# Tying all products of a four in order, and placing the attention steps ahead of other work, in a two-layer transformer kernel

## The chip, the cores and the metric

The kernel runs on one core of one Trainium2 chip. The metric is the device time of one execution in microseconds (us). TensorE is called PE below, its weight loads PEld, VectorE is DVE, ScalarE is ACT, GpSimd is POOL and the queue that starts most transfers is SP.

## The reference, cut to what matters

Two layers work on x of shape (4, 512, 128): four batch rows of 512 tokens with 128 channels, all float32. Each layer adds an attention and a mixture of experts to x, both fed by the same layer norm. Layer 0 has a banded attention (window 64) and 16 gated experts. Layer 1, which the change touches, is this:

```
def _L1_attn_ref(x, w_qkv, w_out):            # x = xn, 16 heads of 8 channels
    q, k, v = split(x @ w_qkv), each to (b, heads, n, 8)
    attn = softmax(q @ k^T / sqrt(128))
    out  = (attn @ v), heads put side by side
    return out @ w_out

def _L1_ffn_ref(x, ...):                      # 8 experts, top 2
    gate = softmax over the two largest scores of relu(x rw1 + rb1) rw2 + rb2
    out  = sum over experts e of gate_e * (relu(x W1_e + b1_e) W2_e + b2_e)

xn = layernorm(x)
x  = x + _L1_attn_ref(xn, ...) + _L1_ffn_ref(xn, ...)
```

## The kernel before, in words

**Layer 0** (`band_logits`, `gated_experts`, `prepare`) fills about the first 946 us. Its banded attention output of the last batch row (`band_values`, lines 304 to 374) and layer 1's experts of the last two batch rows (`relu_experts`, lines 392 to 451) are still to be done then. They run beside layer 1's attention.

**Layer 1's attention** (`full_attention`, lines 769 to 947) handles 16 groups: 4 batch rows times 4 groups of 4 heads. A head has only 8 channels, so each head of a group sits on its own 32 of the 128 rows of PE (q and k tiles of 128 partitions, head h at partitions 32h). Four products that lie on four different sets of 32 rows can be worked on side by side. For a group there are 4 token tiles of 128 rows; each (group, tile, two heads) is a pair, 128 pairs in all. Each pair is needed twice:

- as an "m" product (`score<-k,q`, line 920): q times k, of which DVE takes the row maxima over 128 x 1024 numbers (`nmax`, line 936);
- as an "x" product (`score<-qa,k`, same line): k times q with the negated maxima folded into q (`qa`), of which ACT takes exp over 128 x 1024 numbers (`ex`, line 942).

A step holds one m pair and one x pair, which use complementary head pairs, so that its four products lie on four row sets: this is a four. The x pair lies `AHEAD` = 12 pairs behind the m pair. So there are 6 steps with only m products, 116 mixed steps and 6 with only x products. The first product of a step waits (a Sync dependency) for the maxima and the exp of the step in front, whose PSUM banks it writes.

After every second step `weigh` (line 832) multiplies ex with the values, again four products, here on four column sets (`accbank<-ex,vaug`, line 838). Between the steps lie `queries` and `keys` (lines 810 and 819), `with_maxima` and `normalise` (transposes at line 792), `values`, `turned`, `project_out`, and the experts: `hidden` (line 381, then relu on ACT at line 389), the second expert product (line 442), `part` on DVE (446) and `total` on POOL (447).

**What sets the order.** The kernel is written in program order, and `weave` interleaves the attention with the other track in a fixed ratio of steps. When the program is built, a planner puts the instructions on each engine's queue: on each engine it takes, among those it holds to be ready at that moment of its model, the one with the lowest number, and the number is the place in program order. `tc.high_priority(offset=4000)` lowers the number of what is written inside by 4000. Layer 0's products at line 574 have that already. A manual dependency of class NoSync fixes the order on a queue and adds no wait; one of class Sync adds a wait. The queue that results is fixed; the engine works through it in order.

Before the change the helper `in_order(mm, new)` ties only the first product of a four to the last product that was written before it. The other three of the four are free to be placed whenever the planner picks them. The list `pace`, which `in_order` appends to, also ties each `hidden` product behind the attention product written last.

Of the kernel before, what the change touches and what calls it, by code (L numbers as in the profile page):

```python
# [23 lines left out]
AF = mybir.ActivationFunctionType  # L24
ALU = mybir.AluOpType
AX = mybir.AxisListType
PSUM = bass.MemoryType.PSUM

P = 128
B, T, C = 4, 512, 128  # L30
NT = B * T // P
TPB = T // P
# [65 lines left out]
def two_layers(ctx: ExitStack, tc: tile.TileContext, w: dict, consts: bass.AP, out: bass.AP):  # L98
    nc = tc.nc
# [10 lines left out]
    def accbank():  # L110
        return ps_acc.tile([P, 512], FP, tag="acc", name="accbank")
# [648 lines left out]
    vaug = [one.tile([P, TPB, H, 32], FP, name=f"vaug{i}") for i in range(2)]  # L760
    nmax = [one.tile([P, TPB, 4, 32], FP, name=f"nmax{i}") for i in range(2)]
    for i in range(2):
        nc.gpsimd.memset(vaug[i], 0.0)
        nc.gpsimd.memset(vaug[i][:, :, :, 8:9], 1.0)
        nc.gpsimd.memset(nmax[i], 0.0)

    AHEAD = 12

    def full_attention():
# [4 lines left out]
        inv = 1.0 / math.sqrt(float(C))  # L774
        groups = [(b, g) for b in range(B) for g in range(4)]
        outs, q, k, qa, av, ex = {}, {}, {}, {}, {}, {}
        freed = []
        last = pace

        def in_order(mm, new):  # L780
            if new and last:
                tc.add_manual_dep(
                    mm.ins, last[-1].ins.name,
                    mybir.DependencyInfo(mybir.DependencyClass.NoSync, mybir.DependencyReason.DATA),
                    reason="products of four tiles stay together",
                )
            last.append(mm)
# [44 lines left out]
        def weigh(n, i):  # L832
            b, g = groups[n]
            if i == 0:
                av[n] = accbank()
            for h in range(4):
                r = 32 * h
                mm = nc.tensor.matmul(  # L838
                    av[n][r:r + 32, :], vaug[b % 2][:, i, g * 4 + h, :], ex[n, i][:, h, :],
                    start=(i == 0), stop=(i == TPB - 1),  # L840
                )
                in_order(mm, h == 0)
            if i == TPB - 1:
                avs = work.tile([P, TPB, P], FP, tag="avs1", name="avs1")
                nc.scalar.copy(avs.rearrange("p t n -> p (t n)"), av[n])
                av[n] = avs
# [34 lines left out]
        pairs = [(n, i, two) for n in range(len(groups)) for i in range(TPB) for two in (0, 2)]  # L881
        steps, head = [], AHEAD // 2
        for j in range(head):
            steps.append((pairs[2 * j:2 * j + 2], []))
        m_step = {j: j // 2 for j in range(AHEAD)}
        x_step = {}
        for j in range(AHEAD, len(pairs)):
            x_step[j - AHEAD] = m_step[j] = len(steps)
            n, i, two = pairs[j - AHEAD]
            steps.append(([pairs[j]], [(n, i, 2 - pairs[j][2])]))  # L890
        for j in range(len(pairs) - AHEAD, len(pairs), 2):
            x_step[j] = x_step[j + 1] = len(steps)
            steps.append(([], pairs[j:j + 2]))

        for n, (b, g) in enumerate(groups):
            t = m_step[8 * n]
            at(t - 5 if n > 1 else t - 3, queries, n)
            at(t - 3 if n > 1 else t - 2, keys, n)
            if g == 0:
                at(t + 1, values, b)  # L900
            at(m_step[8 * n + 7] + 1, with_maxima, n)
            for i in range(TPB):
                at(x_step[8 * n + 2 * i + 1] + 1, weigh, n, i)
            t = x_step[8 * n + 7]
            at(t + 3, normalise, n)
            if g == 3:
                at(t + 5, turned, b)
                at(t + 6, project_out, b)

        for t in range(min(todo), max(todo) + 1):  # L910
            ms, xs = steps[t] if 0 <= t < len(steps) else ([], [])
            tags = iter(("m", "x"))
            work_on = []
            before, freed = freed, []
            for kind, (n, i, two) in [("m", p) for p in ms] + [("x", p) for p in xs]:
                ps = ps_q.tile([P, 2, T], FP, tag=next(tags), name="score")
                for h in range(two, two + 2):
                    r = slice(32 * h, 32 * h + 32)
                    own, seen = (q[n], k[n]) if kind == "m" else (k[n], qa[n])
                    mm = nc.tensor.matmul(  # L920
                        ps[:, h - two, :], own[r, i * P:(i + 1) * P], seen[r, :], start=True, stop=True
                    )
                    new = not work_on and h == two
                    in_order(mm, new)
                    if new:

                        for f in before:
                            tc.add_manual_dep(
                                mm.ins, f.ins.name,
                                mybir.DependencyInfo(mybir.DependencyClass.Sync, mybir.DependencyReason.DATA),  # L930
                                reason="products of four tiles stay together",
                            )
                work_on.append((kind, n, i, two, ps))
            for kind, n, i, two, ps in work_on[::-1]:
                if kind == "m":
                    freed.append(nc.vector.tensor_reduce(  # L936
                        nmax[n % 2][:, i, two:two + 2, 8:9], ps, AX.X, ALU.max, negate=True
                    ))
                else:
                    if (n, i) not in ex:  # L940
                        ex[n, i] = ep.tile([P, 4, T], FP, tag="ex", name="ex")
                    freed.append(nc.scalar.activation(ex[n, i][:, two:two + 2, :], ps, AF.Exp, scale=inv))  # L942
            for f, args in todo.get(t, []):
                f(*args)
            if t % 2:
                for _ in range(1 + (t % 8 in (1, 7))):
                    yield

    x_out = out.rearrange("b (t p) c -> p b t c", p=P)
    weave(  # L950
        (full_attention(), 106),
        (after(woven((band_values(B - 1, ready[B - 1][1]), 14), (experts[B - 2], 41)), relu_experts(B - 1)), 13 + 40 + 76 + 4),
    )
# [35 lines left out]
```

## Time and profile before

| | us |
|---|---|
| three runs | 1382.46, 1379.99, 1385.32 |
| median | 1382.46 |
| the profiled execution | 1381.3 |
| its span, first to last instruction | 1379.5 |

The profile covers one execution. Busy shares of the span are PE 85%, PEld 33%, DVE 73%, ACT 74%, POOL 7%. Layer 1's attention begins with the first m product at 946.7 us and the last x product ends at 1366.7 us.

How to read it: each product of the program is two passes on PE, so one product of 512 columns gives two MATMUL records of about 0.6 to 0.7 us. Records overlap, since PE is pipelined; what a pass takes from the stream is the distance from its start to the start of the next. "x2" in a timeline row means two records merged, and the number in front is the time that they cover. The bracket at the end of a row is the idle time of that engine just before it, and what ended it. PEclk is the clock that PE was granted, 1.00 being full speed.

### The profile page before, as it was taken

What the parts mean: (1) busy time and instruction counts of PE and PEld (TensorE: products, weight loads), DVE (VectorE), ACT (ScalarE), POOL (GpSimd) and SP (SyncE); (2) the same over time, 40 slices, a digit from 0 to 9 for tenths busy, and PEclk for the clock granted to TensorE, in tenths of its full rate; (3) what the DMA queues carried; (4) which work ended last, traced back from release to release, by engine and by line L of the source; (5) the groups of instructions that cost most, each with busy time, mean ns of one, the idle gap of its engine ahead of it and who ended that gap; (6) DMA issues with size and microseconds to landing.
All of it is one profiled execution on the core that took longest, in us unless ns stands there. A gap on an engine that the chain in (4) does not pass through costs nothing.

```text
span 1379.5 us, 17426 instructions
## 1 busy us (share of the span) xinstructions
PE 1174.3 (85%) x6763; PEld 450.2 (33%) x6763; DVE 1012.4 (73%) x1085; ACT 1018.5 (74%) x1160; POOL 96.9 (7%) x68
## 2 busy tenths in 40 slices
PE   5676976678889789889989988887999899999997
PEld 2122323123433323353333334232333332333322
DVE  4999998999866999987799998843444434444451
ACT  4899997999968899988889988862454435545554
POOL 2000000000000002200002320012000000000000
PEclk9799998899879999999999999999999989999999
DMA  7121213446212445622244751235133200011100
GB/s 268 44 74 52 76 52 103 100 118 153 62 41 75 150 102 145 170 64 64 73 153 110 180 131 48 67 96 166 49 88 77 69 9 24 24 38 39 31 16 8
DMA packets 168524, 117.61 MB, mean 85 GB/s; under 512 B 66621, under 2 KB 149274, under 8 KB 166906
## 3 DMA queue, kind: packets, MB, share of 16 engines
q1 hardware_dynamic: 166970, 109.77, 29.3%
q0 software_dynamic: 1184, 6.29, 1.2%
q8 instruction: 54, 0.88, 0.3%
q10 hardware_dynamic: 288, 0.43, 0.1%
q14 instruction: 28, 0.23, 0.1%
HBM read 89.00 MB, written 27.46 MB: 84 GB/s over the span
## 4 chain that ended last, share of the span: by engine, by line
PE 59%; ACT 17%; DVE 13%; DMA 6%; issue 5%; SPq 0%; DVEq 0%; ACTq 0%
PE score L920 11%; PE lbank L574 10%; PE bank L381 8%; PE bank L442 7%; ACT z L566 6%; DVE z L560 5%; PE accbank L838 4%; ACT z L562 3%; PE gbank L674 3%; PE accbank L663 3%; DMA wb<-by_s 3%; PE gbank L681 2%; DMA wT<-wT_all 2%; DVE nmax L936 2%; PE abank L810 1%
## 5 line engine op out<-in xcount | busy, mean ns | idle before, releaser
L560 DVE TENSOR_TENSOR z<-proj 128x2044 f32<-128x2044 f32 (+31 forms) x256 | 554.1, 2189 | 29.0 <-PE lbank L574 12.6
L574 PE MATMUL lbank<-z,place 128*32 128x504 f32 (+18 forms) x2048 | 288.9, 639 | 110.1 <-ACT z L566 68.8
L936 DVE TENSOR_REDUCE nmax<-score 128x2 f32<-128x1024 f32 x128 | 156.3, 1225 | 182.3 <-PE score L920 180.1
L566 ACT ACTIVATE z<-z,posb 128x1024 f32<-128x1024 f32 (+31 forms) x256 | 267.3, 1097 | 10.2 <-DVE z L560 8.2
L942 ACT ACTIVATE ex<-score 128x1024 f32<-128x1024 f32 x128 | 130.3, 1023 | 159.7 <-PE score L920 159.7
L562 ACT ACTIVATE z<-z,brep 128x2048 f32<-128x2048 f32 (+31 forms) x128 | 241.4, 1906 | 5.3 <-DVE z L560 4.9
L920 PE MATMUL score<-k,q 32*128 32x512 f32 x512 | 152.2, 655 | 13.9 <-DVE nmax L936 11.7
L447 POOL TENSOR_TENSOR total<-total,part 128x512 f32<-128x512 f32 x32 | 82.6, 2580 | 1038.3 <-DVE part L446 1038.3
L920 PE MATMUL score<-qa,k 32*128 32x512 f32 x512 | 139.7, 648 | 2.1 <-ACT ex L942 2.1
L381 PE MATMUL bank<-xT,ew 128*128 128x512 f32 x256 | 136.2, 626 | 1.6 <-ACT h L389 0.8
L442 PE MATMUL bank<-h,ew 128*128 128x512 f32 x256 | 133.1, 619 | 4.7 <-issue 4.7
L389 ACT ACTIVATE h<-bank,cols 128x512 f32<-128x512 f32 x144 | 97.1, 684 | 45.3 <-PE bank L381 44.6
L574 PEld LDWEIGHTS lbank<-z,place 128*32 128x32 f32 x2048 | 43.0, 112 | 264.2 <-ACT z L566 143.9
L663 PEld LDWEIGHTS accbank<-wT,lin 128*128 128x128 f32 x512 | 72.2, 204 | 60.4 <-issue 34.6
L663 PE MATMUL accbank<-wT,lin 128*128 128x128 f32 x512 | 82.1, 297 | 10.1 <-DVE lin L661 10.1
L674 PE MATMUL gbank<-tT,wT 128*128 128x512 f32 x128 | 72.2, 647 | 17.4 <-DMA wT<-wT_all 16.5
L838 PE MATMUL accbank<-ex,vaug 128*32 128x512 f32 x512 | 70.8, 619 | 0.2 <-ACT ex L942 0.2
L681 PE MATMUL gbank<-tT,wT 128*128 128x512 f32 x128 | 70.6, 635 | 0.0
L920 PEld LDWEIGHTS score<-k,q 32*128 32x128 f32 x512 | 41.2, 187 | 89.0 <-ACT ex L942 44.1
L442 PEld LDWEIGHTS bank<-h,ew 128*128 128x128 f32 x256 | 44.2, 193 | 74.4 <-issue 71.0
L381 PEld LDWEIGHTS bank<-xT,ew 128*128 128x128 f32 x256 | 41.9, 192 | 72.8 <-issue 43.6
L659 DVE SCALAR_TENSOR_TENSOR lin<-lin,r 128x512 f32<-128x512 f32 x64 | 44.5, 695 | 28.6 <-ACT lin L683 28.3
(188 smaller groups left out, 1193.7 us busy)
## 6 DMA issues: line engine op xcount, KB each, us to landing
r<-route SPq DMA_DIRECT2D x96, 256.0 KB, 3.5
ew<-in_L_ffn_W SPq DMA_DIRECT2D x64, 256.0 KB, 3.4
wb<-by_s SPq DMA_DIRECT2D x32, 512.0 KB, 4.1
wT<-wT_all SPq DMA_DIRECT2D x48, 192.0 KB, 3.0
by_t<-e SPq DMA_DIRECT2D x8, 1024.0 KB
f<-by_t SPq DMA_DIRECT2D x128, 64.0 KB, 3.1
by_s<-g SPq DMA_DIRECT2D x16, 512.0 KB, 4.2
wb<-by_s SPq DMA_DIRECT2D x24, 256.0 KB, 3.6
```

The lines of the kernel that those rows point to most:

```text
L381: mm = nc.tensor.matmul(ph, wt[:, c * P:(c + 1) * P], xT[:, b * T:(b + 1) * T], start=True, stop=True)
L442: nc.tensor.matmul(py, old[1][:, c, :], old[0][c], start=(c == 0), stop=(c == 3))
L560: nc.vector.tensor_tensor(z[:, :, :, 0:n], seen, own, ALU.subtract)
L562: nc.scalar.activation(z[:, :, :, 0:n], z[:, :, :, 0:n], AF.Gelu, bias=b_dmg)
L566: last = nc.scalar.activation(z[:, dq, :, 0:n], z[:, dq, :, 0:n], AF.Gelu, bias=posb[:, j:j + 1])
L574: mm = nc.tensor.matmul(ps[q:q + 32, t0:T], place[:, kind, 3 - dd:35 - dd], z[:, dq, hg, 0:n], start=(dd == 0), stop=(dd == 3),)
L663: nc.tensor.matmul(ya[:, i * P:(i + 1) * P], lin[:, i * P:(i + 1) * P], wT[:, 2, :], start=False, stop=(e == E0 - 1 and i == TPB - 1),)
L674: nc.tensor.matmul(pg, wT[:, 0, :], tT, start=True, stop=True)
L838: mm = nc.tensor.matmul(av[n][r:r + 32, :], vaug[b % 2][:, i, g * 4 + h, :], ex[n, i][:, h, :], start=(i == 0), stop=(i == TPB - 1),)
L920: mm = nc.tensor.matmul(ps[:, h - two, :], own[r, i * P:(i + 1) * P], seen[r, :], start=True, stop=True)
L936: freed.append(nc.vector.tensor_reduce(nmax[n % 2][:, i, two:two + 2, 8:9], ps, AX.X, ALU.max, negate=True))
L942: freed.append(nc.scalar.activation(ex[n, i][:, two:two + 2, :], ps, AF.Exp, scale=inv))
```

## The change

It does two things in `full_attention`. First, `in_order` ties every product, not only the first of a four, behind the product written just before it, for the scores and for `weigh`. Second, the score products, the `weigh` products, the maxima on DVE and the exp on ACT are written inside `tc.high_priority(offset=FIRST)` with `FIRST = 4000`. The Sync dependency of the first product of a step is left as it is. No instruction is added or removed.

```
+    FIRST = 4000
...
-        def in_order(mm, new):
-            if new and last:
+        def in_order(mm):
+            if last:
                 tc.add_manual_dep(
                     mm.ins, last[-1].ins.name,
                     mybir.DependencyInfo(mybir.DependencyClass.NoSync, mybir.DependencyReason.DATA),
...
-                mm = nc.tensor.matmul(
-                    av[n][r:r + 32, :], vaug[b % 2][:, i, g * 4 + h, :], ex[n, i][:, h, :],
-                    start=(i == 0), stop=(i == TPB - 1),
-                )
-                in_order(mm, h == 0)
+                with tc.high_priority(offset=FIRST):
+                    mm = nc.tensor.matmul(
+                        av[n][r:r + 32, :], vaug[b % 2][:, i, g * 4 + h, :], ex[n, i][:, h, :],
+                        start=(i == 0), stop=(i == TPB - 1),
+                    )
+                in_order(mm)
...
-                    mm = nc.tensor.matmul(
-                        ps[:, h - two, :], own[r, i * P:(i + 1) * P], seen[r, :], start=True, stop=True
-                    )
+                    with tc.high_priority(offset=FIRST):
+                        mm = nc.tensor.matmul(
+                            ps[:, h - two, :], own[r, i * P:(i + 1) * P], seen[r, :], start=True, stop=True
+                        )
                     new = not work_on and h == two
-                    in_order(mm, new)
+                    in_order(mm)
...
-                    freed.append(nc.vector.tensor_reduce(
-                        nmax[n % 2][:, i, two:two + 2, 8:9], ps, AX.X, ALU.max, negate=True
-                    ))
+                    with tc.high_priority(offset=FIRST):
+                        freed.append(nc.vector.tensor_reduce(
+                            nmax[n % 2][:, i, two:two + 2, 8:9], ps, AX.X, ALU.max, negate=True
+                        ))
...
-                    freed.append(nc.scalar.activation(ex[n, i][:, two:two + 2, :], ps, AF.Exp, scale=inv))
+                    with tc.high_priority(offset=FIRST):
+                        freed.append(nc.scalar.activation(ex[n, i][:, two:two + 2, :], ps, AF.Exp, scale=inv))
```

## The prediction

> **What bounds the kernel now.** The change touches nothing before 946.7 us, so I read that part by stage first: busy time per engine and granted clock in five stretches of layer 1's attention.
>
> ```profile
> core 0: us, PE busy (x) PEld busy (x) DVE busy (x) ACT busy (x) POOL busy (x), PEclk, DMA share, GB/s
> 946.00:970.00 24.00, 16.32 (x76) 6.49 (x77) 14.15 (x14) 3.69 (x6) 0.00 (x0) 0.86 0.51 128
> 970.00:1117.00 147.00, 136.90 (x935) 49.13 (x934) 70.72 (x90) 71.38 (x89) 3.83 (x3) 0.98 0.26 62
> 1117.00:1140.00 23.00, 21.88 (x73) 9.23 (x74) 5.85 (x16) 6.17 (x10) 0.00 (x0) 0.70 0.05 12
> 1140.00:1346.00 206.00, 202.00 (x1096) 64.88 (x1099) 101.13 (x106) 107.38 (x128) 8.89 (x7) 1.00 0.10 29
> 1346.00:1380.00 34.00, 24.39 (x146) 7.95 (x146) 5.08 (x9) 14.30 (x16) 1.28 (x1) 0.90 0.03 8
> ```
>
> From 1140 to 1346 PE is busy 202 of 206 us at full clock, DVE and ACT about half. A busy PE need not be at its peak, so I looked for what PE waits for there (the view of waits, PE alone, same stretch): apart from 0.6 us at one transpose, only this.
>
> ```profile
> PE score L920 <- DVE nmax L936: 3.5, 8, 0.9
> PE score L920 <- ACT ex L942: 0.7, 1, 0.7
> ```
>
> So this stage is bound by PE's stream: it gets shorter by what leaves the stream, not by an earlier maximum. What leaves the stream is seen in PE's timeline.
>
> ```profile
> 1204.02 0.70 PE L920 MATMUL score<-k,q 32*128 32x512 f32 x2
> 1204.03 0.70 PE L920 MATMUL score<-qa,k 32*128 32x512 f32 x2
> ...
> 1205.09 0.66 PE L792 MATMUL abank<-cst,o 128*128 128x128 f32 x4
> 1205.68 1.07 PE L838 MATMUL accbank<-ex,vaug 128*32 128x512 f32 x8
> 1206.67 1.12 PE L920 MATMUL score<-k,q 32*128 32x512 f32 x2
> 1207.72 0.66 PE L792 MATMUL abank<-cst,nmax 128*128 128x128 f32 x4
> 1208.31 0.69 PE L920 MATMUL score<-k,q 32*128 32x512 f32 x1
> 1208.32 0.70 PE L920 MATMUL score<-qa,k 32*128 32x512 f32 x2
> ...
> 1209.38 1.16 PE L868 MATMUL abank<-w_out,oT 128*128 128x128 f32 x8
> ```
>
> The four at 1204.02 holds the stream until 1205.09: 1.07 us. The next is split: one m product alone (1206.67 to 1207.72, 1.05 us), four transposes, then the other three (1208.31 to 1209.38, 1.07 us). A product alone costs as much as a four, so a split costs 1.05 us. The same timeline over the stage shows how a step closes when nothing is put behind `weigh`, and in the last steps, which have x products only:
>
> ```profile
> 1218.50 1.07 PE L838 MATMUL accbank<-ex,vaug 128*32 128x512 f32 x8
> ...
> 1219.98 0.70 PE L920 MATMUL score<-k,q 32*128 32x512 f32 x2 [0.41 <-DVE nmax L936]
> ```
>
> ```profile
> 1362.32 1.14 PE L920 MATMUL score<-qa,k 32*128 32x512 f32 x8 [0.72 <-ACT ex L942]
> ...
> 1363.56 1.94 ACT L942 ACTIVATE ex<-score 128x1024 f32<-128x1024 f32 x2 [1.29 <-PE score L920]
> ...
> 1365.55 0.71 PE L920 MATMUL score<-qa,k 32*128 32x512 f32 x4 [0.72 <-ACT ex L942]
> ```
>
> **The change part by part.** *Tying the four, with priority for its products.* Tying alone would not keep a stranger out; it is the priority that lets the second product win against an older transpose that becomes ready meanwhile. Going through PE's timeline from 946 to 1366 I find split fours at 953.97, 976.49, 1002.36, 1015.72, 1041.17, 1055.44, 1107.76, 1206.67 and 1303.57, each one product first and three later, and one in three parts at 1119.23, 1126.93 and 1131.15. Eight of the nine cost 1.05 each: 8.4. The one at 953.97 lies in the m-only steps, where the maxima set the pace; there the four transposes between (0.58) go too: 1.6. The one in three parts takes 2.01 (half clock) + 1.05 + 2.01 = 5.07 against 2.02 for a four at half clock: 3.0. Sum 13.0 us.
>
> *How much of it reaches the end.* Of the splits, only two lie in the stage that is PE from end to end. Six lie between 970 and 1117, where PE is idle 10 of 147 us, mostly in one wait of 4.34 us for a transfer of `band_values` (1083 to 1087); work saved ahead of it does not shorten the wait by itself, but the attention is then further on, and the experts behind it use the time. I count these at 80% of 13.0, 10.4; bounds 2.1 (the two alone) and 13.0.
>
> *Products placed earlier.* In the PE-bound stage the first m product starts a median of 0.58 us after its maximum ended, and never under 0.15: fours are late by about 0.4 us, because older work goes first. Moving the four forward saves no PE time; it moves fillers behind it. Its price is a wait. The row at 1219.98 shows it: with `weigh` alone between two fours, PE waits for the maximum (1.23) that began when the four ended. `weigh` takes 0.99 of the stream (1205.68 to 1206.67), so the four could have started at 1219.49 and starts at 1219.98: 0.49 lost. Behind the waiting product in PE's queue is everything else, experts first. Four steps of this stage look like that. How many there will be, this trace cannot show: none more, or all `weigh` groups that have something behind them now, 23 of the 35 of this stage and so about 42 of all 64, that is 0 to 20.6 us. I take 6 more, 2.9 us, because of a regularity: four transposes in front of `weigh` are followed by the four at once (7 of 7), `weigh` directly behind the four is followed by one more filler in 19 of 23 cases, and steps without `weigh` mostly have two fillers. The filling is nearly constant, about 1.6 to 2.1 us. That is how it looks if the planner takes the four when it is ready, and it needs no priority for that now.
>
> *Maxima and exp first.* DVE starts a maximum 0.05 us after its product, ACT an exp 0.14 us after (medians from 1140 to 1346). Nothing to gain; 0. What they pass is delayed by at most one of them: a relu (0.69) by an exp (1.02), `part` on DVE by a maximum (1.23), and POOL's `total` behind it. Cover: ACT and DVE are half idle, and POOL waits 254 us of this stage for `part` anyway. Without that cover a relu that is a microsecond late leaves a filler slot empty, 0.4 us; I put it into the 2.9.
>
> *SP and the loads.* No DMA is marked, but expert weights are asked for when their buffers come free, which now is up to one four (1.07) later. They are asked for about one expert (24 to 31 us) ahead and land in 3.4 us (the list of DMA issues): 0. If a load did become late, PE would wait with products queued behind it, as in the 4.34 us above; bound 6.
>
> *The clock.* Here a row and a rule differ. The trace: from 1113.4 to 1117.2 PE ran only six transposes, no gap over 1.06 us, and the products after it took 1.01 us a pass instead of 0.53, seven passes or so, about 3 us lost. The Trainium skill, "TensorE: Matmul & The Clock Gate", section "Why this matters for your kernels", asks only that no idle gap exceed about 3 us. By the rule nothing here would go cold, and earlier products could gain nothing; by the row, a four placed among the transposes and among the 26 small router products (1127.98 to 1131.15, after which a pass took 1.01 again) could keep the clock: up to 6 us. The row decides that the loss exists. Whether a four can be there is another thing: the exp it must wait for stands behind two table loads (1.28 each) for a square root until 1115.03. I take 1 of the 6.
>
> *The tail.* The last steps are ACT's: two exps, 3.22 us a step, and PE idle about 1.1 in each of three steps after the last expert product (1355). Attention further ahead leaves expert products to fill that; bounds 0 and 3.3, I take 1.5.
>
> Sum: −10.4 + 2.9 − 1 − 1.5 = −10.0 us, against the profiled execution's 1381.3 (span 1379.5): 1371.3. The median of the runs is 1.2 higher: 1372.5.
>
> **The rivals.** *Healed, but absorbed.* The splits go, but the six early ones shorten only waits for transfers and for the layer norm of the last row, so 2.1 to 4 us are left: 1379. For it: the stretch 970 to 1140 has chains of transfers (3.9% of the chain in layer 1 is `wb`). Against it: PE work from later is there to fill.
>
> *PE waits at the marked products* (slower). If the planner holds the next four to be ready while `weigh` still runs, priority now places it directly behind, in all of the 42 groups, and PE loses 0.49 in each: +20.6 − 10.4 = +10.2, 1393. It breaks even at 10.4 / 0.49 = 21 groups, and is slower by over 0.5% from 35. For it: four such steps exist. Against it: the regular filling above.
>
> *The ties split the fours.* If a tied product counted as ready only some time after the one in front, fillers would slip in after each: 128 fours by 1.05, +134 us. Against it: the first `weigh` product is tied to the four already, and in the PE-bound stage 23 groups follow the four directly.
>
> *The splits stay*, since something else than order holds the second product: 1382. Against it: in all ten the first product's Sync dependency had covered both banks.
>
> **How the numbers follow.** A measurement of this kernel can tell about 0.5%, 6.9 us, from no change. Main case 0.55, 1362 to 1377 on its own; absorbed 0.20; PE waits 0.17; ties split 0.03; splits stay 0.05. Faster by over 0.5%: 0.47 of the main case and 0.05 of the second, 0.52. Within 0.5%: 0.08 + 0.13 + 0.04 + 0.01, 0.26. Slower: 0.22. The range, from a main case with a clock gain at 1361 to most of the waiting case at 1392, leaves out about 2 in 10.
>
> **What would show it.** Right: every L920 group between 970 and 1346 has eight records together, none of two or six; the waits of L920 for the maxima stay near eight in the PE-bound stage; expert products stand in the gaps of the x-only steps. Wrong: many brackets of 0.4 us at L920, strangers inside the fours, a stretch of experts alone after the last x product, or a new wait of some us for `wb` or expert weights.

## The result, and the profile after

The changed kernel takes 1363.6 us (median of 4 runs) against 1381.2 for the kernel before beside it: ratio 0.9873, 95% interval 0.9835 to 0.9911. Two later comparisons, each on one chip with more runs, gave 0.9909 (0.9888 to 0.9930) and 0.9899 (0.9883 to 0.9914). So it is about 0.9% to 1.3% faster. The profiled execution took 1362.1 us, its span is 1360.3.

**Cut off what the change does not touch.** The two spans differ by 19.2 us, but not all of it is the change. Layer 1's attention begins with the first `queries` product (`abank<-xT,wqk`). It starts at 943.0 us before and at 936.1 after, although PE's queue is the same up to there. In the 13 profiled executions here that have this same queue, that moment lay anywhere from 935.9 to 943.5. What follows it, up to the end of the span, repeats much better. I call it the rest:

| kernel | rest, us, of each profiled execution |
|---|---|
| before | 436.5 |
| ties only (same queues as before) | 438.0 |
| changed | 424.2, 425.0, 424.3 |
| priority for products two to four only | 421.4, 422.2 |
| priority for score products only | 420.5, 421.4 |
| priority for score products only, `wb` products later | 418.8 |

So the change takes about 12 to 13 us off the rest (11.5 to 13.8 between single executions); the other 6 us or so between the first two profiles is the scatter of layer 0. The first two rows are the same program (experiment 1), so 1.5 us between them is scatter too.

The same five stretches as before, moved up by 6.9 us, since the attention starts that much earlier:

```profile
core 0: us, PE busy (x) PEld busy (x) DVE busy (x) ACT busy (x) POOL busy (x), PEclk, DMA share, GB/s
939.10:963.10 24.00, 16.54 (x78) 6.47 (x78) 15.34 (x14) 4.27 (x7) 0.00 (x0) 0.86 0.48 118
963.10:1110.10 147.00, 137.10 (x981) 49.71 (x980) 72.71 (x91) 74.22 (x91) 3.82 (x3) 0.98 0.25 62
1110.10:1133.10 23.00, 22.22 (x115) 8.62 (x108) 10.59 (x20) 10.79 (x14) 0.00 (x0) 0.80 0.04 12
1133.10:1339.10 206.00, 203.92 (x1076) 65.60 (x1072) 94.09 (x102) 107.08 (x128) 8.91 (x7) 1.00 0.09 29
1339.10:1360.30 21.20, 12.94 (x83) 4.72 (x82) 3.07 (x7) 7.52 (x10) 1.26 (x1) 0.97 0.04 13
```

Three things are to be seen. The same 147 us hold more matmul records (981 against 935): the attention is further on. The 23 us around the router have a clock of 0.80 in place of 0.70. The long stretch is PE from end to end as before, and the last stretch ends 12 us sooner (21.2 us against 33.5 to the end of the span): the end has moved, no engine has become faster.

What PE waits for in the long stretch (the view of waits, PE alone):

```profile
PE score L923 <- ACT ex L947: 0.7, 1, 0.7
PE score L923 <- DVE nmax L940: 0.7, 1, 0.7
PE score L923 <- DVE qa L831: 0.5, 1, 0.5
```

Eight waits for the maxima, 3.5 us, have become one of 0.7. And a new kind stands there: a wait for `qa`. PE's timeline shows what it is:

```profile
1190.91 0.70 PE L923 MATMUL score<-k,q 32*128 32x512 f32 x2
1190.93 0.70 PE L923 MATMUL score<-qa,k 32*128 32x512 f32 x2
...
1193.46 1.13 PE L923 MATMUL score<-k,q 32*128 32x512 f32 x4
1194.52 0.66 PE L793 MATMUL abank<-cst,nmax 128*128 128x128 f32 x4
1195.01 1.02 PE L442 MATMUL bank<-h,ew 128*128 128x512 f32 x2
1196.51 1.13 PE L923 MATMUL score<-qa,k 32*128 32x512 f32 x4 [0.47 <-DVE qa L831]
1197.56 1.06 PE L840 MATMUL accbank<-ex,vaug 128*32 128x512 f32 x8
```

At 1190.91 the four is whole. The next one is split in the middle: its m pair runs at 1193.46 alone, and its x pair must wait for `qa`, whose transposes (L793, of `with_maxima`) come only then. These transposes have no priority, so the products have overtaken the work that they need. There are four such splits (m pairs at 1055.14, 1142.39, 1193.46 and 1266.59); the ten of before are gone.

A late `qa` also costs time where no stranger comes between. Here the weight load of the x pair waits for it (the bracket at PEld), and PE with it:

```profile
1169.38 1.09 PE L923 MATMUL score<-k,q 32*128 32x512 f32 x3
...
1169.88 0.30 PEld L923 LDWEIGHTS score<-qa,k 32*128 32x128 f32 x4 [0.21 <-DVE qa L831]
1169.88 0.70 PE L923 MATMUL score<-qa,k 32*128 32x512 f32 x2
...
1170.94 1.06 PE L840 MATMUL accbank<-ex,vaug 128*32 128x512 f32 x8
```

This four holds the stream for 1.56 us (1169.38 to 1170.94) in place of 1.07. Five fours look like this (1169.38, 1219.22, 1243.31, 1293.84, 1317.06), 2.5 us in all. All nine places, the four splits and the five holds, are the first x pair of a group of heads, the first that needs the new `qa`. Together they cost 4.2 + 2.5 = 6.7 us.

**The ledger.** I summed the distances from the start of each matmul record to the start of the next, over the rest, and put what lies beyond a record's own end, less the 0.06 us by which records overlap when PE runs back to back, down as idle. The score products took 152.7 us of PE's stream before and 147.1 after, that is −5.6; everything else of the stream −3.0; idle time went from 36.4 to 32.7. Together −12.3. The −5.6 is the difference of two larger terms: −12.5 for the ten healed splits (experiment 3) and +6.9 for the late `qa`.

### The profile page after: what moved, and what is told of

It reads as the page before. It is cut to its first block, busy times and chain, and to the rows that moved or that the text cites. A ratio compares the mean times of both kernels' runs of the same rounds, so it can differ in the third digit from the quotient of the medians.

```text
span 1360.3 us, 17428 instructions
## 1 busy us (share of the span) xinstructions
PE 1161.7 (85%) x6763; PEld 447.2 (33%) x6763; DVE 1012.0 (74%) x1085; ACT 1019.6 (75%) x1160; POOL 96.9 (7%) x68
## 4 chain that ended last, share of the span: by engine, by line
PE 59%; ACT 17%; DVE 12%; DMA 6%; issue 6%; SPq 0%; POOLq 0%; POOL 0%; DVEq 0%
PE lbank L574 11%; PE score L923 10%; PE bank L381 8%; ACT z L566 7%; PE bank L442 7%; DVE z L560 5%; PE accbank L840 4%; PE gbank L674 3%; ACT z L562 3%; PE accbank L663 3%; PE gbank L681 2%; DMA wT<-wT_all 2%; DMA wb<-by_s 2%; DVE nmax L940 2%; PE bank L235 1%
## 5 line engine op out<-in xcount | busy, mean ns | idle before, releaser
L574 PE MATMUL lbank<-z,place 128*32 128x504 f32 (+18 forms) x2048 | 294.2, 649 | 106.7 <-ACT z L566 64.5
L923 PE MATMUL score<-k,q 32*128 32x512 f32 x512 | 141.0, 655 | 11.1 <-DVE nmax L940 8.4
L674 PE MATMUL gbank<-tT,wT 128*128 128x512 f32 x128 | 71.2, 639 | 16.1 <-DMA wT<-wT_all 15.4
L681 PE MATMUL gbank<-tT,wT 128*128 128x512 f32 x128 | 67.2, 607 | 0.0
L923 PEld LDWEIGHTS score<-k,q 32*128 32x128 f32 x512 | 38.3, 186 | 80.7 <-ACT ex L947 39.4
```

Of the source, the lines that this page charges most:

```text
L574: mm = nc.tensor.matmul(ps[q:q + 32, t0:T], place[:, kind, 3 - dd:35 - dd], z[:, dq, hg, 0:n], start=(dd == 0), stop=(dd == 3),)
L674: nc.tensor.matmul(pg, wT[:, 0, :], tT, start=True, stop=True)
L923: mm = nc.tensor.matmul(ps[:, h - two, :], own[r, i * P:(i + 1) * P], seen[r, :], start=True, stop=True)
```

## The experiments

**1. The ties alone.** All four `with tc.high_priority(offset=FIRST)` taken out of the changed kernel, `in_order(mm)` kept.

```
-                with tc.high_priority(offset=FIRST):
+                if True:
...   (the same at the other three)
```

> The change with its ties and without its priorities. Theory A (the priority heals the fours, a tie alone keeps no stranger out): the same as before, about 1381 us, with the ten split fours in the same places. Rival (the tie is what keeps the four together): the splits go and the time falls by 6.5 to 13 us, to about 1370.

Measured: 1377.0 against 1377.3, ratio 1.0 (0.9986 to 1.0014). As built, its queues are those of before, instruction for instruction, on all five engines. A tie says what comes after what, not that nothing may come between. The same comparison of the queues shows that priority for the maxima and exp alone, with the ties of before, also leaves every queue as it was, and that leaving these two out of the change gives the queues of the changed kernel. So of the change only the priority of the products acts, together with the ties. These two variants were compared as built and not run.

**2. The priority alone.** The changed kernel with the old ties (`in_order(mm, new)`, first products only).

> The change with its priorities and with the ties of before (only the first product of a four is tied). Theory A (healed fours are the gain, and priority needs the ties, since weigh and score products of equal rank can mix): groups of weigh or score products come apart in some 25 to 40 places at about 1.05 us each, so about 1385 to 1400 us. Rival (priority alone does it, the ties are idle): the time of the changed kernel, 1364.

Measured: 1409.7, ratio 1.0248 (1.0223 to 1.0273), 32 us slower than before, and slower than the 1385 to 1400 expected. PE's timeline at one of the bad places:

```profile
1238.78 1.04 PE L840 MATMUL accbank<-ex,vaug 128*32 128x512 f32 x2
1239.76 0.69 PE L923 MATMUL score<-k,q 32*128 32x512 f32 x1
1239.76 0.69 PE L923 MATMUL score<-qa,k 32*128 32x512 f32 x1
...
1240.81 1.05 PE L840 MATMUL accbank<-ex,vaug 128*32 128x512 f32 x2
1241.79 1.12 PE L923 MATMUL score<-qa,k 32*128 32x512 f32 x2
```

One `weigh` product alone (two passes, x2), two score products, one `weigh` product, one score product: each holds the stream for about 1 us, as a whole four would. When everything of a step has the same priority, the untied products of `weigh` and of the score mix. Elsewhere the four is only shuffled (m, x, m, x), and that costs nothing: it takes 1.08. Compared with the changed kernel, the score products take 28.2 us more of the stream and `weigh` 15.6, and the rest is 45.5 longer. So each half of the change needs the other; the rival, that the ties are idle, falls.

**3. Whole fours at their old places.** All products tied; only the second to fourth have priority, the first keeps its place in program order.

```
-                    with tc.high_priority(offset=FIRST):
+                    with tc.high_priority(offset=FIRST if work_on or h > two else 0):
                         mm = nc.tensor.matmul(
                             ps[:, h - two, :], ...
...
-                with tc.high_priority(offset=FIRST):
+                with tc.high_priority(offset=FIRST if h else 0):
                     mm = nc.tensor.matmul(
                         av[n][r:r + 32, :], ...
...   (maxima and exp without priority)
```

> Ties on all products; only the second to fourth product of each four has priority, the first one keeps its place in program order, and maxima and exp keep theirs. All fours are whole, but they start as late as before, behind older work. Theory A (the gain is the healed fours alone): ten splits at 1.05 and a little more, so 10 to 13 us less than before, about 1370, or a few us under that since no new split is made. Rival B (the gain is that whole steps are placed earlier, ahead of transposes and of the router): at most a third of the gain, 1376 or more.

Measured: 1361.2 against 1377.3, ratio 0.9886 (0.9867 to 0.9905). The rest is 421.4, the score products take 140.2 us of the stream: 12.5 less than before (11.2 in the second execution of this kernel), which is close to the prediction's price of the ten splits (13.0). The stretch of the new split in the changed kernel, in this one:

```profile
1191.67 0.70 PE L923 MATMUL score<-k,q 32*128 32x512 f32 x2
1191.68 0.70 PE L923 MATMUL score<-qa,k 32*128 32x512 f32 x2
...
1192.74 1.06 PE L840 MATMUL accbank<-ex,vaug 128*32 128x512 f32 x8
1193.74 1.12 PE L811 MATMUL abank<-xT,wqk 128*128 128x512 f32 x2
1194.79 0.70 PE L923 MATMUL score<-k,q 32*128 32x512 f32 x2
1194.81 0.70 PE L923 MATMUL score<-qa,k 32*128 32x512 f32 x2
```

Since the first product waits its turn in program order, `qa` is there when it runs, and all 128 fours are whole. Its waits for the maxima in the long stretch:

```profile
PE score L923 <- DVE nmax L940: 1.9, 5, 0.4
```

Rival B, that placing whole steps earlier makes the gain, falls: without any of that the whole gain is here. Nor does the changed kernel itself start its fours earlier: in its long stretch the first m product starts a median of 0.58 us after its maximum ended, which is what the prediction counted before the change.

**4. The changed kernel again**, unedited, beside these three.

> The changed kernel once more, on the same chip as the three others: 1364 us, 17 us under before. Its profile tells how much of the 6 us by which layer 0 ended earlier belongs to the run: if that is chance, layer 0 ends at other times here (928 to 936 us at the first product of layer 1's attention) by some us; if it is a property of the changed program, again near 936 against 943 before.

Measured: 1365.2 against 1377.3, ratio 0.9909. Layer 1 starts at 940.2 in its profile, 4.1 us later than in the first one of the same kernel; the rest is 425.0 against 424.2. The 6 us of layer 0 are chance.

**5. Splits made on purpose.** `weigh` does not run at its place but inside the next four, between the first product and the other three.

```
         def weigh(n, i):
+            held.append((n, i))
+
+        def weigh_now(n, i):
...
                     if new:
                         for f in before:
                             tc.add_manual_dep(
...
+                        while held:
+                            weigh_now(*held.pop(0))
```

> The changed kernel, with each weigh group moved from behind its four into the next four, between the first product and the other three: about 60 fours are split on purpose, nothing is added. It measures the price of a split. Theory A (a lone product holds the stream as long as a four, 1.05 us, and PE is the bound nearly everywhere): 60 x 1.05 = 63 us more than the changed kernel, about 1425. Rival (much of a split is hidden, because PE has waits to fill or the three others run beside their neighbours): 30 us or less, 1395 or under.

Measured: 1490.3 against 1378.1, ratio 1.0825 (1.0795 to 1.0856), about 125 us more than the changed kernel and twice what theory A expected, four times the rival's bound. The timeline has the form that was meant:

```profile
1209.08 1.12 PE L928 MATMUL score<-k,q 32*128 32x512 f32 x2
1210.13 1.06 PE L845 MATMUL accbank<-ex,vaug 128*32 128x512 f32 x8
1211.12 0.69 PE L928 MATMUL score<-k,q 32*128 32x512 f32 x1
1211.13 0.70 PE L928 MATMUL score<-qa,k 32*128 32x512 f32 x2
...
1212.19 1.12 PE L381 MATMUL bank<-xT,ew 128*128 128x512 f32 x2
```

The lone product takes 1.05 (1209.08 to 1210.13). 58 of them stand in the trace, 55 of them m products, and m products take 54.1 us more of the stream than in the changed kernel, about 0.98 each, a little more without the late `qa` that it has itself. That part is as theory A had it. But the rest is 130 us longer, and the other 76 us are not the price of a split. The second m product now comes after `weigh`, so the maximum, and with it the next four, starts 2 us later: PE's idle time in the rest grows from 32.7 to 67.6, that is 35 us. The other 41 us are in other products, no more in number but slower: PE runs at half clock for 114 us of the rest, against 27 in the changed kernel. Two kernels, the stretch from 1130 to 1330 of the changed one and from 1150 to 1350 of this one:

```profile
1130.00:1330.00 200.00, 198.72 (x1040) 63.97 (x1040) 95.22 (x105) 102.34 (x122) 8.91 (x7) 0.99 0.10 30
```

```profile
1150.00:1350.00 200.00, 184.62 (x774) 59.46 (x778) 71.60 (x85) 74.90 (x91) 5.08 (x4) 0.89 0.07 22
```

In these 200 us the granted clock is at half in six stretches of 3.4 to 13.7 us. Five of them begin 0.4 to 2.2 us after the end of a wait of 1.4 to 1.6 us; the longest, at 1153.0, begins at the end of the router's small products, with no wait in front. One of the five:

```profile
1189.73 0.49 PE L799 MATMUL abank<-w_qkv,xT 128*128 128x128 f32 x2 [1.55 <-DVE qa L831]
1190.15 1.73 PE L928 MATMUL score<-k,q 32*128 32x512 f32 x2
...
1194.69 1.06 PE L928 MATMUL score<-k,q 32*128 32x512 f32 x1
```

The passes from there on take 1.06 where others take 0.59, until 1200.8.

**6. More slack for `qa`.** `AHEAD = 14` in the changed kernel.

> The changed kernel with AHEAD = 14 in place of 12, so that the x products have one more step of slack behind with_maxima, whose transposes have no priority. One more step with m products only at the start, one more with x products only at the end. Theory A (the four fours that the change still splits are x pairs waiting for qa, which with_maxima delivers late, and cost 1.06 each): no split mixed four, 4.2 us less than the changed kernel, about 1360. Rival (the longer start and end, whose steps take 3.2 to 3.6 us against 3.0, eat it): 1364 or more.

Measured: 1367.3, ratio 0.9924 (0.9901 to 0.9946): not faster than the changed kernel. The step that was aimed at did happen: no mixed four is split (one is still held for `qa`, at 1063.68), and PE's stream is 4.2 us shorter (387.3 against 391.5). But idle time grew by 9.8 us. Half of it is a wait that was already there (view of waits, PE, from 963 to 1125 us; first the changed kernel, then this one):

```profile
PE bank L348 <- DMA wb<-by_s: 4.2, 1, 4.2
```

```profile
PE bank L348 <- DMA wb<-by_s: 9.1, 4, 4.3
```

Another 3.0 us is what the rival named, the longer end: from the first four with x products only to the end of the span it is 34.0 us here and 31.0 in the changed kernel. So the splits were worth about what theory A said, and two other costs ate it.

I read the longer wait so: the queue puts the products of `band_values` where the planner takes their transfer to have landed, and when the attention in front of them gets shorter, they stand at the head of PE's queue before their data. Experiment 12 tests only that more distance shortens the wait.

**7. `with_maxima` with a priority of its own**, behind the products and ahead of all else.

```
+            with tc.high_priority(offset=FIRST // 2):
                 pt = columns(nmax[n % 2].rearrange("p t h e -> p t (h e)"))
                 qa[n] = work.tile([P, T], FP, tag="qa", name="qa")
                 nc.vector.tensor_tensor(qa[n], pt, q[n], ALU.add)
```

> The changed kernel, with with_maxima (transposes and the sum into qa) at a priority of 2000, behind the products and ahead of all other work. If lateness in the planner's order alone splits the last four fours, they should all be whole: 4.2 us less. In the queue as built three of the four stay split, so what holds qa is not rank but the one abank bank or nmax itself: then 1 us less than the changed kernel, within its noise.

Measured: 1370.4, ratio 0.9946 (0.9925 to 0.9967), a miss: some 5 to 6 us slower than the changed kernel where 1 to 4 less was expected. The stream is 2.5 us shorter, idle time 8.1 longer: the waits for `wb` at L348 are 8.0 us, and PE now also waits for `nmax` with the transposes themselves (3.3 us, in three waits, at L793, from 963 to 1125). A likely reading is that a transpose of high rank is put in the queue as soon as the planner holds the maxima to be ready, and everything behind it waits when they are not. Three splits stand in this trace, but not all at the old places: two are where the changed kernel has them, the third where it only held the x pair, and one old split has become such a hold. Why these stay is open.

**8. Priority for the score products alone**, ties on all.

> Ties on all products, priority for the score products alone; weigh, maxima and exp keep program order. The score fours are all whole, some three weigh groups come apart, and the next four stands directly behind weigh in about twice as many places as before (29 against 15). Theory A with the price of the prediction (0.49 us of waiting where nothing lies between weigh and the next four, 1.05 for a weigh group that comes apart): -12 for the whole fours, +7 for 14 more waits, +3 for weigh, so 2 us under before. Rival (such waits cost nothing, since the work that is passed fills later gaps): 9 us or more under before.

Measured: 1360.4, ratio 0.9877 (0.9853 to 0.9902); the rival was right. The score products take 139.9 us of the stream, and `weigh`, of which three groups come apart, 69.4 (66.5 before): the −12 and the +3 of theory A are there. The +7 is not. The next four does stand directly behind `weigh` in 29 places, but in 27 of them other work has gone in front of `weigh`, so the maximum has had its time. Only in two does `weigh` stand alone between two fours, and there PE waits 0.47 us, as priced; the gaps in all 29 places sum to 1.9 us.

**9 to 12. Side by side on one chip.** The changed kernel, experiments 8 and 3 again, and experiment 8 with one pause more in `band_values`, in layer 1 only (the step counts given to `weave` are raised to match, from 14 to 22 and from 13 + 40 to 21 + 40):

```
                         in_=bass.AP(by_s.tensor, at, [[H * BW - 1, P], [BW, 8], [1, n]]),
                     )
+                if pace:
+                    yield
                 for g4 in range(2 * half, 2 * half + 2):
```

> The changed kernel on the same chip as the three others, so that they can be compared with it directly: 12 to 17 us under before.

> Priority for the score products alone, once more, beside the changed kernel. Theory A (the gain is whole fours; the changed kernel still splits four at about 1.05 and this one none): 4 us under the changed kernel. Rival (that difference came from the chips of the earlier calls): no difference over 2 us.

> Priority for the second to fourth product alone, once more, beside the changed kernel. If whole fours are all that counts, the same as score_prio_2 within 2 us and 4 us under the changed kernel, although here the fours keep their late places and there they do not.

> score_prio with one more pause of the program order between the loads of wb and the products that need them, so that these products stand further back in PE's queue. It asks what the wait of about 4 us in front of them costs, which all kernels so far have near 1080 us: with the half-speed passes after it about 6 us. If the wait only needs distance: 4 to 6 us under score_prio_2. If the experts of the last row, which start behind this chain, become late by as much: no gain.

Measured, before being 1375.9:

| kernel | us | ratio, interval |
|---|---|---|
| changed | 1362.7 | 0.9899 (0.9883 to 0.9914) |
| score products only | 1361.7 | 0.9894 (0.9873 to 0.9914) |
| products two to four only | 1362.3 | 0.9893 (0.9876 to 0.991) |
| score products only, `wb` products later | 1358.9 | 0.9866 (0.9848 to 0.9885) |

The times cannot tell the first three apart, so the 4 us expected between them are not confirmed by time. The rest of their profiles (424.3, 421.4, 422.2) puts the two without new splits 2 to 3 us ahead; over all executions in the table of rests it is 2.0 to 4.5. The last kernel has the lowest time of all, but its interval still touches those of the others, and the 4 to 6 us expected are not reached: it is 2.8 us under experiment 8 by the times, its rest is 2.6 us shorter (1.7 against the other execution). The wait that it was made for, from 1060 to 1130 us, first in experiment 8 beside it, then here:

```profile
PE bank L348 <- DMA wb<-by_s: 4.3, 1, 4.3
```

```profile
PE bank L350 <- DMA wb<-by_s: 1.5, 1, 1.5
```

## Why the prediction was right, and which terms were off

Forecast: 10.0 us less, a median of 1372.5. Measured: 12 to 13 less in the part that the change touches, 12 to 18 by the times; the median is 1363.6. The mechanism, that split fours are what leaves PE's stream, is shown by experiment 3, where the score products' stream falls by 12.5 us and the time with it, and the price of a split by experiment 5. Experiments 1 and 2 show that ties and priority are both needed. That the sum came so close is partly luck: a discount of 2.6 us that was not needed and a term of +2.9 with the wrong sign stand against a term of 6.7 that the prediction put at nothing. The terms:

- **The price of the ten splits, 13.0 us.** Right: 12.5 in experiment 3 (11.2 in its second execution). The discount to 80% was wrong. Experiment 3 brings the whole of it to the end, 14 to 17 us of the rest, although six of the splits lie where PE also waits for transfers; what makes up the 2 to 4 us beyond the splits is open. "The experts behind it use the time" was the better half of that paragraph.
- **No new splits.** The missing term. I went through what the priority is moved past, but not what the moved products themselves need: `with_maxima` keeps its old rank. Four fours came apart at `qa`, at 1.06 each, and five were held in the middle, at 0.49 each: 6.7 us. The sign "every L920 group has eight records together" failed there. Experiment 6 confirms the cause: with one more step of slack for `qa` no split and a single hold are left.
- **Products placed earlier, +2.9.** Wrong sign. In the long stretch the waits for the maxima fell from 3.5 to 0.7 us. `weigh` has priority too, so it now stands directly behind its four, and the transposes that used to stand in front of it fill the time behind it. In the changed kernel no four stands directly behind a `weigh` group. The regular filling that the prediction leaned on was real, but I let only the fours move and not `weigh`. It is the other way round: `weigh` moved, and the fours start as long after their maxima as before.
- **The clock, −1.** Around the router PE was at half clock for 6.8 and 6.8 us before (in both executions of that program) and for 3.4 and 6.8 after (in all three): 1.7 us of full speed. (The 0.80 in place of 0.70 in the two rows makes 2.3, because the rows cut these stretches at different points.) Right in sign, taken a little low. Four fours do stand among the router's products now (1113.95 to 1124.67), yet the second stretch at half clock is as long as before.
- **The tail, −1.5.** Did not come. From the first four with x products only to the end it is 31.0 us after (1329.33 to 1360.3) and was 30.1 before (1349.42 to 1379.5). Two expert products fill gaps there, but two did so before as well (1351.48 and 1354.71). A third now runs behind the last x product, and what follows it on PE has to wait 1.74 us for the experts' sum (two rows below the list). In experiments 3 and 8, where no expert product is left over, the same part takes 29.2 us. (Of the 30.1 before, 0.9 is half clock in the last products, `abank<-w_out,oT`: 2.08 in place of 1.16.) The bound of 3.3 was also too wide: the waits of the three steps that the prediction took for 1.1 each are 0.62, 0.72 and 0.72.
- **Maxima and exp, 0; SP, 0.** Right. The maxima's and exp's priority changes no queue at all.

The third expert product of the tail, and the wait behind it:

```profile
1349.87 1.13 PE L442 MATMUL bank<-h,ew 128*128 128x512 f32 x2
...
1353.17 0.66 PE L235 MATMUL bank<-cst,total 128*128 128x128 f32 x4 [1.74 <-POOL total L447]
```

The slower rival, PE waiting at 21 groups or more, did not come, by the view of waits above. "Healed, but absorbed", with 2.1 to 4 us, did not either: about 12 us reach the end. Nor did "the ties split the fours"; it is the priority without the ties that splits them (experiment 2).

## What to carry to other kernels

In an engine's stream that is full, count what each group holds, and look for groups that are broken by a stranger: here a lone product of a packed four cost as much as the four (1.05 us against 1.07). To keep a group together it takes both an order inside it and a rank that lets its later members win; in this kernel either alone did nothing or harm, and it was enough to give the rank to the members after the first. When a consumer is moved ahead, move what it needs as well, and look afterwards for the waits that the shorter queue uncovers, here at a transfer that had not landed when the products that need it stood at the head of the queue.

## What the runs showed of the hardware

The unexpected part is how much a small wait spreads. In experiment 5 the 58 lone products explain 54 us and the rest grew by 130. In the 200 us shown there, five waits of 1.4 to 1.6 us were each followed, within 2.2 us, by 3.4 to 10.2 us at half clock, where a pass takes 1.06 us in place of 0.59; the mean granted clock of that stage was 0.89. Not every such wait is followed so: one of 1.41 us at 1336.11 was not. In the changed kernel, whose waits between 1133.7 and the end of its last x product at 1346.8 stay under 0.8 us, the clock was full all that time.

The first 940 us, with one and the same PE queue, scatter by 7.6 us from run to run, the 420 to 440 us behind them by 1.5 at most for the same queues, though from two or three executions each. Comparing the part behind a common mark told kernels apart that their times could not.
